# Where the small arithmetic of a layer normalisation runs: eight operations on GpSimd in the place of six on VectorE around one on GpSimd, in a four-layer graph kernel

## The chip, the cores and the metric

The kernel runs on one core of a Trainium2 chip. What counts is the device time of one execution in microseconds: 1110.71 us before the change, the median of three runs (1109.0 to 1111.08). In the profile the engines are PE (TensorE, with PEld for its weight loads), DVE (VectorE), ACT (ScalarE), POOL (GpSimd) and SP (SyncE, which issues transfers). L118 is line 118 of the kernel before.

## What is computed

A graph of 2708 nodes with 128 features each (x) and a sparse weighted adjacency (adj, 2708 × 2708) goes through four layers. Each layer is wrapped in the same way:

```
h = maximum(layernorm(x), 0)
x = x + layer(h)            # layers 0 to 3

layernorm(x) = (x - mean(x)) / sqrt(var(x) + 1e-5)     # over the 128 features of a node
```

- Layer 0: the transposed adjacency times h, over the degree.
- Layer 1: message passing. `gelu(s[i] + d[j] + b)` is weighted by `adj[i, j]` and summed over j, joined to h, taken through a linear map and gelu, added to h and normalised again with `ln_w` and `ln_b`.
- Layer 2: `adj @ h`, a linear map with relu, and a GRU cell.
- Layer 3: attention with two heads over the pattern of adj. Its input is normalised once more, and for each head `atten @ h + x` is normalised before a last linear map and elu; the heads are averaged.

So a node is normalised seven times: before each of the four layers, at the end of layer 1, at the start of layer 3's attention, and in layer 3 once for each head (two in one set of instructions).

## The kernel before

The nodes lie in 22 tiles of 128 rows (the last has 20), taken in groups of up to four: six groups, the last with two tiles. A row tile is [128 rows on partitions, 128 features]. x stays in on-chip memory as `xs`.

**A normalisation.** `moments` (L109–120) takes up to four row tiles: for each, VectorE computes mean and variance (`bn_stats`, `bn_aggr`, L116–117) into `mv` [128, k, 2]. L118 (VectorE) adds epsilon to the k variances, and L119 (GpSimd) raises that to the power −0.5. `factors` (L122–130) refines the result by one Newton step and makes the shift, −mean × rstd, with five instructions of VectorE (L125–129) on [128, k]. `scale_rows` (L132–135) then lets ScalarE write each row tile as func(scale × row + shift). The tiles `st`, `mv` and `r` come from the pool `small` with three buffers for each name. `moments` and `factors` are called apart, so that other work of VectorE lies between them while GpSimd takes the power:

- n0, before layer 0: `normalise` (L140), for the six groups one after another at the start.
- n1, before layer 1: `enter` adds layer 0's result to xs and calls `moments`; `rows` calls `factors` and `scale_rows` later.
- n1u, at the end of layer 1, and n2, before layer 2: steps 2–3 and 5–6 of `update` (L567–585); step 4 scales and lets GpSimd multiply by ln_w and add ln_b (L579).
- n3, before layer 3, and n3z, in its attention: in `finish_chunk` (L1023–1031), once for each of the six groups.
- n4, in layer 3: in `close` (L886–890), for two row tiles and both heads, twelve times.

In the trace the tiles of n0, n1, n2, n3 and n4 are all called n_r and n_mv; those of the other two n1u_r and n3z_r.

**The order of the work.** Layer 0 (0 to 245 us) is ordered by a scheduler: SyncE fetches rows of adj as `a`, TensorE multiplies them with h (L220) and transposes them (L249), and VectorE finds the nonzeros of each row in 22 blocks of 124 columns with `max` and an index search (L240, L241). GpSimd prepares for each tile the blocks at the diagonal (`near`, `dg`, L229–234). From there on the order is written by hand. The prologue of layer 1 (245 to 305) is a list of steps and tiles; `enter`, `rows` and `turn_rows` stand in it among steps that build the lists (L339 compares a list with a count, 128 x 2816). Layer 1 itself (to 640) runs in periods of one tile each: TensorE picks and sums (L499, L503, L524), ScalarE takes gelu, GpSimd and ScalarE write the matrices `put` (L423, L431), and `updates(t)` puts one step of an `update` in each period.

In layer 2 (to 860) TensorE multiplies chunks of 512 columns of the transposed adjacency with h (L959). At each piece, VectorE makes 0/1 masks of most row tiles and GpSimd of the rest (L951, L954). A generator, `finish_chunk`, lies over the products of the next chunk; its `yield n` means: go on after n more units of TensorE's work. The same holds for `close` in layer 3 (860 to 1108), which lies over the products of the attention: VectorE makes the weights (L806, 128 x 1024 in the wide runs), TensorE multiplies (L838), and a close divides by the sums and adds h (L884), normalises (n4), transposes (L894), multiplies (L903) and ends with elu, for which GpSimd runs L915–917 and VectorE L920–921.

Of the kernel before, what the change touches and what calls it, by code (L numbers as in the profile page):

```python
# [22 lines left out]
AF = mybir.ActivationFunctionType  # L23
ALU = mybir.AluOpType
# [15 lines left out]
EPS = 1e-5  # L40
# [20 lines left out]
def listed_layers(ctx: ExitStack, tc: tile.TileContext, x, adj, w, out, flag):  # L61
    nc = tc.nc
# [10 lines left out]
    xs = const.tile([P, NT, D], F32, name="xs")  # L73
    h = const.tile([P, NT, D], F32, name="hs")
# [31 lines left out]
    minus_half = const.tile([P, 8], F32, name="minus_half")  # L106
    nc.vector.memset(minus_half, -0.5)

    def moments(src, name, pool=small):  # L109

        k = len(src)
        st = pool.tile([P, k, 6], F32, name=name + "_st")
        mv = pool.tile([P, k, 2], F32, name=name + "_mv")
        r = pool.tile([P, 4, k], F32, name=name + "_r")
        for q in range(k):
            nc.vector.bn_stats(st[:, q, :], src[q])  # L116
            nc.vector.bn_aggr(mv[:, q, :], st[:, q, :])
        nc.vector.tensor_scalar(r[:, 3, :], mv[:, :, 1], EPS, None, ALU.add)  # L118
        nc.gpsimd.tensor_tensor(r[:, 0, :], r[:, 3, :], minus_half[:, 0:k], ALU.pow)  # L119
        return mv, r  # L120

    def factors(mv, r):  # L122

        rstd, shift, tmp, ve = (r[:, q, :] for q in range(4))
        nc.vector.tensor_tensor(tmp, rstd, rstd, ALU.mult)  # L125
        nc.vector.tensor_tensor(tmp, tmp, ve, ALU.mult)
        nc.vector.tensor_scalar(tmp, tmp, -0.5, 1.5, ALU.mult, ALU.add)
        nc.vector.tensor_tensor(rstd, rstd, tmp, ALU.mult)
        nc.vector.scalar_tensor_tensor(shift, mv[:, :, 0], -1.0, rstd, op0=ALU.mult, op1=ALU.mult)
        return rstd, shift  # L130

    def scale_rows(dst, src, rstd, shift, func):  # L132

        for q in range(len(src)):
            nc.scalar.activation(dst[q], src[q], func, bias=shift[:, q : q + 1], scale=rstd[:, q : q + 1])

    def tiles_of(v, t, k):
        return [v[:, t + q, :] for q in range(k)]

    def normalise(dst, src, t, k, func, name):  # L140

        rows = tiles_of(src, t, k)
        scale_rows(tiles_of(dst, t, k), rows, *factors(*moments(rows, name)), func)

    def span(t, k):

# [50 lines left out]
    with tc.tile_pool(name="l0c", bufs=1) as fix:  # L197
# [4 lines left out]
        with (  # L202
# [6 lines left out]
            for gi, (g0, gk) in enumerate(GROUPS):  # L209
# [4 lines left out]
                for q in range(gk):  # L214
                    n = g0 + q
                    m = size(n)
# [27 lines left out]
                for j in range(NT):  # L244
                    k = size(j)
                    p = bank("p_T")
                    for q in range(gk):
                        m = size(g0 + q)
# [52 lines left out]
    with (  # L301
# [27 lines left out]
        state = {}  # L329
# [215 lines left out]
        ups = {}  # L545

        def update(g, step):
            t, k = GROUPS[g]
            if step == 0:
                u = work.tile([P, 4, D], F32, name="u1")  # L550
                p = rpool.tile([P, CH], F32, tag="r", name="p_u")
                agg = aggs.pop(g)
                if size(t + k - 1) < P:
                    nc.vector.memset(u[:, k - 1, :], 0.0)
                for q in range(k):
                    m, c = size(t + q), (t + q) * P
                    pq = p[0:m, q * D : (q + 1) * D]
                    nc.tensor.matmul(pq, hT[:, c : c + m], upd_wT[:, 0, :], start=True, stop=False)
                    nc.tensor.matmul(pq, agg[:, q, 0:m], upd_wT[:, 1, :], start=False, stop=True)
                pv = p.rearrange("p (t d) -> p t d", t=4)  # L560
                bv = upd_b.unsqueeze(1).to_broadcast([P, 4, D])
                whole = k if size(t + k - 1) == P else k - 1
                nc.vector.tensor_tensor(u[:, 0:whole, :], pv[:, 0:whole, :], bv[:, 0:whole, :], ALU.add)
                if whole < k:
                    nc.vector.tensor_tensor(u[0:TAIL, whole, :], pv[0:TAIL, whole, :], upd_b[0:TAIL, :], ALU.add)
                ups[g] = [u]
            u = ups[g][0]  # L567
            rows = tiles_of(u, 0, k)
            if step == 1:
                nc.scalar.activation(u[:, 0:k, :], u[:, 0:k, :], AF.Gelu)  # L570
            if step == 2:
                nc.vector.tensor_tensor(u[:, 0:k, :], u[:, 0:k, :], h[:, t : t + k, :], ALU.add)  # L572
                ups[g].append(moments(rows, "n1u"))
            if step in (3, 6):
                ups[g].append(factors(*ups[g].pop()))
            if step == 4:
                scale_rows(rows, rows, *ups[g].pop(), AF.Identity)
                for v, op in ((ln_w, ALU.mult), (ln_b, ALU.add)):
                    nc.gpsimd.tensor_tensor(u[:, 0:k, :], u[:, 0:k, :], v.unsqueeze(1).to_broadcast([P, k, D]), op)  # L579
            if step == 5:  # L580
                nc.vector.tensor_tensor(xs[:, t : t + k, :], xs[:, t : t + k, :], u[:, 0:k, :], ALU.add)
                ups[g].append(moments(tiles_of(xs, t, k), "n2"))
            if step == 7:
                scale_rows(tiles_of(h, t, k), tiles_of(xs, t, k), *ups[g].pop(), AF.Relu)
                ups.pop(g)
# [75 lines left out]

        def rows(g):
            t, k = GROUPS[g]
            scale_rows(tiles_of(h, t, k), tiles_of(xs, t, k), *factors(*state.pop(("m", g))), AF.Relu)

        def turn_rows(g):
            t, k = GROUPS[g]
# [207 lines left out]
    def close(run, sums, first):  # L875

        res, inv3 = sums
        k0 = min(2, run[1] - first)
        t0 = run[0] + first
        n = 2 * k0  # L880
        att = out_pool.tile([P, 4, D], F32, name="att_s")
        for s in range(n):
            i = s % 2 * run[1] + first + s // 2
            nc.vector.scalar_tensor_tensor(  # L884
                att[:, s, :], res[:, i, 0:D], inv3[:, i : i + 1], h3[:, t0 + s // 2, :], op0=ALU.mult, op1=ALU.add
            )  # L886
        rows = tiles_of(att, 0, n)
        mv = moments(rows, "n4")
        yield 4.5
        scale_rows(rows, rows, *factors(*mv), AF.Identity)  # L890
        yield 4
        p = bank("p_aT")
        for s in range(n):
            nc.tensor.transpose(p[:, s * P : (s + 1) * P], att[:, s, :], ident)  # L894
        spend(0.25 * n)
        zT = out_pool.tile([P, 4, P], F32, name="z4T")
        nc.scalar.activation(
            zT[:, 0:n, :], p.rearrange("p (s i) -> p s i", s=4)[:, 0:n, :], AF.Identity, bias=shift2, scale=gain2
        )
        yield 1.5  # L900
        p = bank("p_o")
        for s in range(n):
            nc.tensor.matmul(  # L903
                p[:, s * D : (s + 1) * D], zT[:, s, :], ff1T[:, s % 2 * D : (s % 2 + 1) * D], start=True, stop=True
            )
        spend(0.33 * n)

        v = p.rearrange("p (q k d) -> p q k d", q=2, k=2)[:, 0:k0, :, :]
        el = out_pool.tile([P, 2, 2, D], F32, name="el")[:, 0:k0, :, :]
        po = out_pool.tile([P, 2, 2, D], F32, name="po")[:, 0:k0, :, :]  # L910
        nc.scalar.activation(el, v, AF.Relu, scale=-1.0)
        nc.scalar.activation(po, v, AF.Relu, scale=0.5)
        nc.scalar.activation(el, el, AF.Exp, scale=-1.0)
        less = out_pool.tile([P, 2, D], F32, name="less")
        nc.gpsimd.tensor_scalar(less[:, 0:k0, :], xs[:, t0 : t0 + k0, :], -1.0, None, ALU.add)  # L915
        nc.gpsimd.tensor_tensor(po[:, :, 0, :], po[:, :, 0, :], po[:, :, 1, :], ALU.add)
        nc.gpsimd.tensor_tensor(less[:, 0:k0, :], less[:, 0:k0, :], po[:, :, 0, :], ALU.add)
        yield 6
        y = out_pool.tile([P, 2, D], F32, name="y")
        nc.vector.tensor_tensor(el[:, :, 0, :], el[:, :, 0, :], el[:, :, 1, :], ALU.add)  # L920
        nc.vector.scalar_tensor_tensor(  # L921
            y[:, 0:k0, :], el[:, :, 0, :], 0.5, less[:, 0:k0, :], op0=ALU.mult, op1=ALU.add
        )
        for q in range(k0):
            m, i = size(t0 + q), (t0 + q) * P
            nc.sync.dma_start(out[i : i + m, :], y[0:m, q, :])
# [7 lines left out]
    with (  # L934
# [30 lines left out]
        def finish_chunk(t0, k0, pa):  # L965
# [8 lines left out]
            for t in range(t0, t0 + k0):  # L974
                m = size(t)
# [37 lines left out]
            for q in range(k0):  # L1013
                m = size(t0 + q)
# [8 lines left out]
            x_rows, h_rows = tiles_of(xs, t0, k0), tiles_of(h3, t0, k0)  # L1023
            mv = moments(x_rows, "n3")
            yield 6
            scale_rows(h_rows, x_rows, *factors(*mv), AF.Relu)
            yield 2
            mv = moments(h_rows, "n3z")
            yield 4
            z = zpool.tile([P, 4, D], F32, name="z3")  # L1030
            scale_rows(tiles_of(z, 0, k0), h_rows, *factors(*mv), AF.Identity)
            yield 4
            zT = zpool.tile([D, CH], F32, name="z3T")
            turn(
# [11 lines left out]
            for q in range(k0):  # L1046
                t = t0 + q
# [509 lines left out]
```

## Time and profile before

| what | before |
|---|---|
| time | 1110.71 us (1109.0 to 1111.08) |
| span of the profile | 1108.1 us |
| clock granted to TensorE | 0.933 |
| instructions of GpSimd | 466 |
| L118, n_r, 128 x 4 or 2 | 36, mean 178 ns |
| L125 to L129, n_r | 36 each, means 235, 198, 337, 233, 202 ns |
| L119, n1u_r and n3z_r, 128 x 4 | 5 and 5, means 1248 and 1768 ns |
| L806, weights of layer 3 | 176, 160.0 us |
| L423, put on GpSimd | 176, 147.7 us |

The page's second part cuts the span into 40 slices of 27.7 us. A digit is the busy share of a slice in tenths:

```profile
PE   3998887944389999999999979999979999999993
DVE  5999999997766668676887255655578977997673
POOL 4111111103385655776566253344310200340132
```

VectorE is full in slices 2 to 9, layer 0; TensorE in nearly all that come after the eleventh. A wait that the trace names stands in brackets behind a row of the timeline, as the idle time of the engine ahead of the instruction and what ended it.

### The profile page before, as it was taken

How to read it: one execution, taken by the hardware profiler on the slowest of the kernel's cores; microseconds unless marked ns; L12 is line 12 of the kernel's file. 1: busy time of each engine (PE TensorE's matmuls, PEld its weight loads, DVE VectorE, ACT ScalarE, POOL GpSimd, SP SyncE). 2: the span in 40 equal slices, each digit the busy share in tenths (PEclk: the TensorE clock that was granted, in tenths of full speed). 3: DMA queues.
4: the chain of work that ended last, by engine and by line, in shares of the span. 5: the costliest groups of instructions: out<-in, count | busy, mean ns of one | idle time of the engine just before them, and what ended most of it. 6: DMA issues, size and time to landing. Idle time of an engine off the chain costs nothing. (4 is left out here: it accounts for less than half of the span.)

```text
span 1108.1 us, 21904 instructions
## 1 busy us (share of the span) xinstructions
PE 963.6 (87%) x7968; PEld 760.1 (69%) x7968; DVE 839.4 (76%) x2948; ACT 504.2 (46%) x1319; POOL 394.1 (36%) x466
## 2 busy tenths in 40 slices
PE   3998887944389999999999979999979999999993
PEld 1455444523389999999898934444468899999772
DVE  5999999997766668676887255655578977997673
ACT  3857556623476666656676521433322200230142
POOL 4111111103385655776566253344310200340132
PEclk9999889755699999999999989999989999999996
DMA  9488978522133222322222056545300000000000
GB/s 361 164 299 281 324 259 288 178 64 68 46 106 102 96 86 90 106 86 101 83 103 80 28 193 209 190 157 198 100 18 1 1 9 1 1 20 1 2 15 14
DMA packets 55298, 125.39 MB, mean 113 GB/s; under 512 B 7414, under 2 KB 19782, under 8 KB 52472
## 3 DMA queue, kind: packets, MB, share of 16 engines
q1 hardware_dynamic: 48590, 121.12, 31.6%
q10 hardware_dynamic: 6590, 2.77, 1.0%
q8 instruction: 64, 1.05, 0.4%
q14 instruction: 54, 0.44, 0.1%
HBM read 77.30 MB, written 30.84 MB: 98 GB/s over the span
## 5 line engine op out<-in xcount | busy, mean ns | idle before, releaser
L838 PE MATMUL att<-hv,wt 128*128 128x129 f32 (+2 forms) x1936 | 240.7, 281 | 9.2 <-DVE wt L806 9.2
L838 PEld LDWEIGHTS att<-hv,wt 128*128 128x128 f32 (+2 forms) x1936 | 221.8, 190 | 26.2 <-DVE wt L806 9.1
L806 DVE SCALAR_TENSOR_TENSOR wt<-row,lift,mask 128x1024 f32<-128x1024 f32 (+5 forms) x176 | 160.0, 939 | 34.2 <-PE att L838 34.2
L423 POOL TENSOR_SCALAR put<-mine,value 128x128 f32<-128x128 bf16 x176 | 147.7, 855 | 72.4 <-DVE mine L339 70.0
L499 PE MATMUL p_m<-s,sel 128*128 128x128 bf16 x1452 | 160.8, 219 | 5.4 <-ACT g L511 5.4
L119 POOL TENSOR_TENSOR n_r<-n_r,minus_half 128x4 f32<-128x4 f32 (+1 forms) x36 | 51.3, 1425 | 316.1 <-DVE n_r L118 305.2
L503 PE MATMUL p_m<-d,cols 124*128 124x128 bf16 (+1 forms) x1452 | 161.0, 219 | 1.4 <-DVE cols L453 1.3
L220 PE MATMUL acc<-a,hs 128*128 128x512 f32 (+2 forms) x264 | 122.3, 599 | 27.6 <-DMA a<-in_adj 18.9
L524 PE MATMUL agg<-put,g 128*128 128x128 f32 (+1 forms) x968 | 135.8, 281 | 0.0
L241 DVE FIND_INDEX8 col<-val,a 128x8 uint16<-128x124 f32 (+1 forms) x441 | 118.6, 280 | 0.0
L959 PE MATMUL p_agg<-a,hs 128*128 128x512 f32 (+2 forms) x264 | 111.5, 564 | 7.7 <-DVE u L572 4.8
L524 PEld LDWEIGHTS agg<-put,g 128*128 128x128 f32 x968 | 118.1, 192 | 0.0
L499 PEld LDWEIGHTS <-sel 128*128 128x128 bf16 x1452 | 103.7, 97 | 10.8 <-issue 7.1
L503 PEld LDWEIGHTS <-cols 124*128 124x128 bf16 (+1 forms) x1452 | 101.8, 97 | 1.9 <-DVE cols L453 1.9
L240 DVE MAX8 val<-a 128x8 f32<-128x124 f32 (+1 forms) x441 | 102.6, 272 | 0.0
L511 ACT ACTIVATE g<-p_m 128x512 f32<-128x512 f32 x132 | 73.0, 553 | 63.6 <-PE p_m L503 63.6
L431 ACT ACTIVATE put<-mine,value 128x128 f32<-128x128 bf16 x308 | 100.5, 390 | 0.0
L220 PEld LDWEIGHTS acc<-a,hs 128*128 128x128 f32 (+1 forms) x264 | 49.7, 209 | 72.2 <-issue 43.4
L249 PEld LDWEIGHTS p_T<-ident,a 128*128 128x128 f32 x484 | 59.0, 146 | 52.8 <-ACT aT L253 25.4
L249 PE MATMUL p_T<-ident,a 128*128 128x128 f32 x484 | 77.7, 293 | 18.3 <-DMA a<-in_adj 10.0
L253 ACT ACTIVATE aT<-p_T 128x512 f32<-128x512 f32 (+2 forms) x132 | 70.9, 541 | 40.0 <-issue 16.3
L959 PEld LDWEIGHTS p_agg<-a,hs 128*128 128x128 f32 (+1 forms) x264 | 48.6, 196 | 56.6 <-issue 55.1
(228 smaller groups left out, 1396.6 us busy)
## 6 DMA issues: line engine op xcount, KB each, us to landing
a<-in_adj SPq DMA_DIRECT2D x21, 1354.0 KB
adjT<-aT SPq DMA_DIRECT2D x105, 256.0 KB
a<-adjT SPq DMA_DIRECT2D x20, 1280.0 KB
spread<-passed SPq DMA_DIRECT2D x22, 704.0 KB
later<-sel SPq DMA_DIRECT2D x22, 616.0 KB
later<-sel SPq DMA_DIRECT2D x22, 82.5 KB
adjT<-aT SPq DMA_DIRECT2D x21, 74.0 KB
a<-adjT SPq DMA_DIRECT2D x4, 370.0 KB
```

The source lines that it names most:

```text
L220: nc.tensor.matmul(accs[ci][:, 0:cw], h[0:m, n, :], a[0:m, c : c + cw], start=(n == 0), stop=(n == NT - 1))
L240: nc.vector.max(val[:, n, b, :], ab)
L241: nc.vector.max_index(col[:, n, b, :], val[:, n, b, :], ab)
L249: nc.tensor.transpose(p[0:k, q * P : q * P + m], a4[0:m, q, j * P : j * P + k], ident[0:m, 0:m])
L423: nc.gpsimd.tensor_scalar(st["put", 0][:, b, :], st["mine"][:, b, :], st["value"][:, b : b + 1], None, ALU.mult)
L431: nc.scalar.activation(st["put", 1][:, b - HP, :], st["mine"][:, b, :], AF.Identity, scale=st["value"][:, b : b + 1])
L499: nc.tensor.matmul(p[:, b - b0, :], st["sel"][:, b, :], s3[:, q, t % 2, :], start=(q == 0), stop=False)
L503: nc.tensor.matmul(p[:, b - b0, :], st["cols"][0:kb, b, :], d3[0:kb, b, q, :], start=False, stop=(q == 2))
L524: nc.tensor.matmul(agg, g[:, b - 4 * k, :], put, start=(b == 0), stop=False)
L806: nc.vector.scalar_tensor_tensor(wt[0:kj, :], row[0:kj, k, c : c + n], lift[0:kj, j, k : k + 1], mask[0:kj, j, c : c + n], op0=ALU.max, op ...
L838: nc.tensor.matmul(banks[s // 3][0:m, s % 3, :], wt[0:kj, q * P : q * P + m], hv[0:kj, j, k, :], start=(v < 2 and s // 3 not in touched), ...
L959: nc.tensor.matmul(pa[:, 0:n], h[0:k, j, :], a[0:k, j - j0, 0:n], start=(j == 0), stop=(j == NT - 1))
```

## The change

`moments` now also does the work of `factors`, all of it on GpSimd, and hands back scale and shift: add epsilon, power, three instructions that form 1.5 − 0.5 × rstd² × (var + eps), the multiplication with it, mean × rstd, and the sign. VectorE's combined last instruction (L129) becomes two of GpSimd. `factors` and its calls disappear; `scale_rows` stands where it stood. The purpose is to take small dependent instructions off VectorE and to have one crossing from VectorE to GpSimd and one from there to ScalarE, in the place of VectorE to GpSimd to VectorE to ScalarE. Each GpSimd instruction waits for the one before it on GpSimd's own semaphore.

```diff
@@ moments
-        nc.vector.tensor_scalar(r[:, 3, :], mv[:, :, 1], EPS, None, ALU.add)
-        nc.gpsimd.tensor_tensor(r[:, 0, :], r[:, 3, :], minus_half[:, 0:k], ALU.pow)
-        return mv, r
-
-    def factors(mv, r):
 
         rstd, shift, tmp, ve = (r[:, q, :] for q in range(4))
-        nc.vector.tensor_tensor(tmp, rstd, rstd, ALU.mult)
-        nc.vector.tensor_tensor(tmp, tmp, ve, ALU.mult)
-        nc.vector.tensor_scalar(tmp, tmp, -0.5, 1.5, ALU.mult, ALU.add)
-        nc.vector.tensor_tensor(rstd, rstd, tmp, ALU.mult)
-        nc.vector.scalar_tensor_tensor(shift, mv[:, :, 0], -1.0, rstd, op0=ALU.mult, op1=ALU.mult)
+        nc.gpsimd.tensor_scalar(ve, mv[:, :, 1], EPS, None, ALU.add)
+        nc.gpsimd.tensor_tensor(rstd, ve, minus_half[:, 0:k], ALU.pow)
+        nc.gpsimd.tensor_tensor(tmp, rstd, rstd, ALU.mult)
+        nc.gpsimd.tensor_tensor(tmp, tmp, ve, ALU.mult)
+        nc.gpsimd.tensor_scalar(tmp, tmp, -0.5, 1.5, ALU.mult, ALU.add)
+        nc.gpsimd.tensor_tensor(rstd, rstd, tmp, ALU.mult)
+        nc.gpsimd.tensor_tensor(shift, mv[:, :, 0], rstd, ALU.mult)
+        nc.gpsimd.tensor_scalar(shift, shift, -1.0, None, ALU.mult)
         return rstd, shift
@@ normalise; rows, close and finish_chunk (n3, n3z) in the same way
-        scale_rows(tiles_of(dst, t, k), rows, *factors(*moments(rows, name)), func)
+        scale_rows(tiles_of(dst, t, k), rows, *moments(rows, name), func)
@@ update
-            if step in (3, 6):
-                ups[g].append(factors(*ups[g].pop()))
```

More of the change, by code (lines that the diff above doesn't have):

```diff
@@ L663, in rows @@
             t, k = GROUPS[g]
-            scale_rows(tiles_of(h, t, k), tiles_of(xs, t, k), *factors(*state.pop(("m", g))), AF.Relu)
+            scale_rows(tiles_of(h, t, k), tiles_of(xs, t, k), *state.pop(("m", g)), AF.Relu)
         def turn_rows(g):
@@ L889, in close @@
         yield 4.5
-        scale_rows(rows, rows, *factors(*mv), AF.Identity)
+        scale_rows(rows, rows, *mv, AF.Identity)
         yield 4
@@ L1025, in finish_chunk @@
             yield 6
-            scale_rows(h_rows, x_rows, *factors(*mv), AF.Relu)
+            scale_rows(h_rows, x_rows, *mv, AF.Relu)
             yield 2
@@ L1030, in finish_chunk @@
             z = zpool.tile([P, 4, D], F32, name="z3")
-            scale_rows(tiles_of(z, 0, k0), h_rows, *factors(*mv), AF.Identity)
+            scale_rows(tiles_of(z, 0, k0), h_rows, *mv, AF.Identity)
             yield 4
```

## The prediction

> **What bounds the kernel now.** I read the page first (busy shares, slices), then busy time by stage, then rows, waits and timelines of the stages where the change sits. From the page:
>
> ```profile
> PE 963.6 (87%) x7968; PEld 760.1 (69%) x7968; DVE 839.4 (76%) x2948; ACT 504.2 (46%) x1319; POOL 394.1 (36%) x466
> L806 DVE SCALAR_TENSOR_TENSOR wt<-row,lift,mask 128x1024 f32<-128x1024 f32 (+5 forms) x176 | 160.0, 939 | 34.2 <-PE att L838 34.2
> L119 POOL TENSOR_TENSOR n_r<-n_r,minus_half 128x4 f32<-128x4 f32 (+1 forms) x36 | 51.3, 1425 | 316.1 <-DVE n_r L118 305.2
> ```
>
> GpSimd looks idle (36%), but that is an average. Busy time by stage (start and end, length, then busy us of each engine):
>
> ```profile
> 0.00:245.00 245.00, 187.51 (x756) 108.31 (x757) 232.06 (x1568) 145.50 (x338) 39.27 (x83) 0.89 0.71 250
> 245.00:305.00 60.00, 24.69 (x144) 19.10 (x144) 47.41 (x154) 23.82 (x57) 17.61 (x21) 0.59 0.17 57
> 305.00:640.00 335.00, 323.08 (x4506) 312.26 (x4503) 233.35 (x455) 215.90 (x628) 208.89 (x262) 1.00 0.26 88
> 670.00:800.00 130.00, 129.11 (x352) 59.93 (x351) 74.62 (x207) 45.95 (x113) 50.64 (x31) 1.00 0.51 170
> 860.00:1084.00 224.00, 220.09 (x1799) 202.23 (x1798) 179.04 (x333) 44.10 (x92) 48.34 (x42) 0.98 0.02 6
> ```
>
> Layer 0 (to 245) is bound by VectorE (232 of 245); the prologue of layer 1 (245 to 305) is a latency chain that VectorE dominates; everything from 305 to 1084 is bound by TensorE, except 640–670 and 800–860. Only the first two can sell a VectorE saving; in the others only a longer chain counts, and only where its slack ends. A normalisation in layer 2, from the timeline at 690 us (start, length, row):
>
> ```profile
> 690.13 0.17 DVE L118 TENSOR_SCALAR n_r<-n_mv 128x4 f32<-128x4 f32 x1
> 690.20 1.22 DVE L951 TENSOR_SCALAR mask<-a 128x2048 uint8<-128x2048 f32 x1
> 690.38 1.93 POOL L119 TENSOR_TENSOR n_r<-n_r,minus_half 128x4 f32<-128x4 f32 x1 [10.85 <-DVE n_r L118]
> 692.35 0.57 DVE L125 TENSOR_TENSOR n_r<-n_r 128x4 f32<-128x4 f32 x1 [0.92 <-POOL n_r L119]
> 693.55 0.16 DVE L129 SCALAR_TENSOR_TENSOR n_r<-n_mv,n_r 128x4 f32<-128x4 f32 x1
> ```
>
> and in layer 3, beside the weights L806:
>
> ```profile
> 870.49 0.17 DVE L118 TENSOR_SCALAR n_r<-n_mv 128x4 f32<-128x4 f32 x1
> 870.56 2.48 DVE L806 SCALAR_TENSOR_TENSOR wt<-row,lift,mask 128x1024 f32<-128x1024 f32 x2
> 870.74 1.97 POOL L119 TENSOR_TENSOR n_r<-n_r,minus_half 128x4 f32<-128x4 f32 x1 [30.27 <-DVE n_r L118]
> 873.74 0.16 DVE L129 SCALAR_TENSOR_TENSOR n_r<-n_mv,n_r 128x4 f32<-128x4 f32 x1
> 874.58 0.30 PE L894 MATMUL p_aT<-ident,att_s 128*128 128x128 f32 x1 [0.58 <-ACT att_s L135]
> ```
>
> The power takes 1.93–1.97 us here; three in a row with VectorE off the memory took 3.23 (12.72–15.95), so 1.01 is its own. It gets going only as the VectorE instruction that started before it ends (691.42; 871.80), and then needs some 0.9.
>
> **What the Trainium skill says.** "SBUF — State Buffer", "Who interferes with whom": GpSimd's port pair is shared with VectorE; an instruction of VectorE with two inputs in SBUF, or a tensor_scalar in a two-port mode, and a reading one of GpSimd shut each other out whole, by issue order. The trace agrees (1.01 becomes 1.93 and 1.97). "GPSIMD Engine Reference", "3.1 Elementwise", has two dispatch hops on GpSimd against one on VectorE; the trace has no tiny GpSimd multiply, but one of 128x20 takes 0.23 us and VectorE's of 128x4 take 0.16.
>
> **The change part by part.** *Removed:* six VectorE instructions (118, 125–129) in each of 48 normalisations (36 whose tile is called n_r, six n1u_r, six n3z_r), 288 in all, some 60 us of busy time; 0.15–0.17 us each where nothing disturbs them, five at a pitch of 0.20, so about 1.2 us per normalisation, and one crossing back from GpSimd to VectorE. *Added:* GpSimd's add ahead of the power and six instructions behind it, each waiting for the one before. Step: below by VectorE's pitch, 0.20; above by 0.40 (a 128x128 tensor_scalar, 0.53, less some of its size). I take 0.27: the 128x20 multiply's 0.19–0.23 and the 0.04–0.08 us seen between dependent GpSimd instructions (916 to 917: 0.08). Alone, a chain is 0.2 + 1.01 + 6 × 0.27 = 2.8, and with the start 3.1 us; before, 0.17 + 0.1 + 1.01 + 5 × 0.2 + gaps = 2.5. *Moved:* outside layer 0 the order on TensorE, ScalarE and the queues is as before; whatever stood behind the power on GpSimd now stands behind the chain.
>
> By stage:
> - Layer 0: the chains run while VectorE does lists. VectorE saves six sets of small instructions (those of groups 3–5 lie between list instructions at a pitch of some 0.1, so 18 × 0.1 = 1.8), their waits for the power (0.74, 0.67, 0.36) and a step blocked to 18.62; but its first block maxima wait for near and dg, which stand behind three chains on GpSimd. The first hs goes from 19.46 to about 26, which TensorE's slack (11.8 us of waiting at the end) takes. −1.5 (−4 to +1).
> - Prologue: six groups × 1.1 us leave VectorE, but ScalarE takes rows in order, behind copies that wait for other VectorE work, so little of it arrives; and group 5's factors no longer stand behind L339 (297.21 to 298.83); still L339 has two inputs and holds up the rest of that chain. TensorE waits 30.7 us for hs in all. −1.5 (−4 to +1).
> - Layer 1, 305–640: a chain in GpSimd's queue delays the puts (L423) by 3 us; GpSimd waits 70 us there for mine, and no product waits for a put (0.0), so it is hidden. −0.5.
> - 640–670: behind one another on GpSimd stand the chains of n1u of group 5 and n2 of group 4, then ln_w and ln_b of group 5, the memset of score (657.07) and the masks; the masks release the pieces of adjT that TensorE waits for at 665.7. Two chains less two powers, 3.4, less the VectorE part that was on this way: +2.1 (0 to +4).
> - Layer 2: n3 above lasts 690.10 to 693.71 = 3.6. After: the mask to 691.35, then 2.8 = 694.15: +0.45. n3z follows on it with the same +0.5 and, by the rest of a mask, 0.1 more. TensorE waits for z already at p_z (0.24 at 701.57) and is in order: 1.1 × 4 chunks = +4.5 (+1 to +7).
> - 800–860: the mask of 20x148 comes behind a chain (+1.7 to L977 and the weights); relief of VectorE gives 2.2. −0.5 (−3 to +2).
> - Layer 3: in the first close the bn_aggr ends at 870.45; the weights hold the first step to 871.8 and the power to 873.0 (done 873.9); with the factors gone VectorE goes on with two more weights, so steps 3 and 4 get in at 874.3 and 875.5, the last four by 876.6, against 873.90: +2.7, and TensorE already waits 0.58. The same walk gives +0.8, 0, 0, +2, +2.7 for the next closes and 0 for the later ones, which have 1.4–3.6 us of slack: 8.2 if each step is held up so. I take two thirds, since VectorE pauses for TensorE (34.2 us): +5.5 (0 to +9).
> - Tail, where nothing hides anything: the last but one chain starts when its bn_aggr ends (1087.05) and, with some 0.4 us behind two-input work, ends near 1090.2, about where L129 does (1090.47); the last (128x2, power 0.70) can only start then and takes 0.2 + 0.7 + 6 × 0.27 = 2.5 to 1092.7, against 1091.61 before: +1 (0 to +2).
>
> Sum: −1.5 − 1.5 − 0.5 + 2.1 + 4.5 − 0.5 + 5.5 + 1 = +9.1: 1119.8 us.
>
> **The rivals.** *Relief wins.* For: VectorE is full in layer 0 (232 of 245) and the prologue, and a crossing goes. Against: a third of the saving only lies there. With −4 and −4 there, −2 in 800–860, +1, +2 and +1 in 640–670, layer 2 and layer 3, and −0.5 and +1 as above, −6.5: 1104. *A draw.* Steps at 0.20 and chains that slip into VectorE's pauses: 640–670 +1, layer 2 +2, layer 3 +1, the rest as above: +1.0, so 1111.7. *Shut out everywhere.* All eight steps wait for a VectorE instruction, 8 × 1.24 = 10 us beside weights, and in the closes with slack too: layer 3 +15, layer 2 +6, the rest as above: +20, so 1131. For it: the power does so in every close; against: L916 and L917 take 0.84 and 0.86 where 0.72 is their own, so many get through.
>
> **How the numbers follow.** The forecast 0.53, shut out 0.13, relief 0.19, draw 0.15. Faster 0.20, same 0.15, slower 0.65. The range runs from 1105, near relief's 1104, to 1130, near shut-out's 1131; half of each of these cases, 0.09 and 0.07, lies beyond. My ends of the stages would sum to a wider span, but they won't all fall on one side.
>
> **What would show it.** GpSimd's steps at 0.27 pitch where VectorE is quiet; n3 and n3z 0.5 us longer each and p_z's wait 1 us longer per chunk; the chain of the first close over 5.5 us and p_aT 2–3 us later; VectorE some 60 us less busy and TensorE's busy time the same. I am wrong if steps take 0.4 or more (then 1125 and up), if the first hs at 26 us is more than layer 0 can take back, or if layer 0 and the prologue end 5 us or more sooner.

## The result, and the profile after

The changed kernel takes 1122.26 us (median of four runs, 1120.11 to 1125.58) against 1110.76 before: a ratio of 1.0109, 95% interval [1.008, 1.0138], so some 12 us slower (9 to 15). Forecast were +9.1 us and 1105 to 1130. Runs of one kernel spread by a few us, and a profile shows one of them; that of the changed kernel is its longest, 1125.58 us (span 1123.7 against 1108.1 in the profile before). All shifts below that come from a profile are shifts of that run.

The page of the changed kernel, rows that answer to those shown of the kernel before (L802 is L806 before; L120 is the chain's first step):

```profile
PE 977.3 (87%) x7968; PEld 769.0 (68%) x7968; DVE 786.0 (70%) x2660; ACT 504.5 (45%) x1319; POOL 485.6 (43%) x802
L802 DVE SCALAR_TENSOR_TENSOR wt<-row,lift,mask 128x1024 f32<-128x1024 f32 (+5 forms) x176 | 158.1, 925 | 48.5 <-PE att L834 48.5
L120 POOL TENSOR_SCALAR n_r<-n_mv 128x4 f32<-128x4 f32 (+1 forms) x36 | 22.4, 623 | 278.0 <-DVE n_mv L117 271.7
```

VectorE is 53 us less busy, GpSimd 92 us more. TensorE has the same 7968 products, and yet 13.7 us more of busy time: a first sign of something the forecast didn't have. By stage, in the columns of before (start and end, length, busy us of each engine, granted clock, share of transfers, GB/s):

```profile
0.00:245.00 245.00, 188.57 (x750) 108.60 (x750) 227.03 (x1530) 144.00 (x330) 47.00 (x125) 0.89 0.70 248
245.00:305.00 60.00, 28.24 (x150) 20.64 (x151) 41.51 (x119) 25.52 (x67) 29.36 (x63) 0.56 0.20 64
305.00:640.00 335.00, 324.31 (x4513) 313.60 (x4512) 226.85 (x407) 216.65 (x632) 231.26 (x318) 1.00 0.26 88
670.00:800.00 130.00, 126.86 (x324) 58.13 (x324) 59.95 (x157) 39.90 (x102) 58.74 (x78) 0.97 0.51 174
860.00:1084.00 224.00, 219.32 (x1794) 205.22 (x1793) 170.09 (x283) 38.70 (x86) 61.17 (x98) 0.97 0.02 5
```

In layer 2 the clock is 0.97 where it was 1.00. A normalisation there, from the timeline of the changed kernel (first chunk; L947 is L951 before, L133 is L135):

```profile
691.58 1.19 DVE L947 TENSOR_SCALAR mask<-a 128x2048 uint8<-128x2048 f32 x1
691.74 1.11 POOL L120 TENSOR_SCALAR n_r<-n_mv 128x4 f32<-128x4 f32 x1 [10.05 <-DVE n_mv L117]
692.94 1.03 POOL L121 TENSOR_TENSOR n_r<-n_r,minus_half 128x4 f32<-128x4 f32 x1
694.05 0.20 POOL L122 TENSOR_TENSOR n_r<-n_r 128x4 f32<-128x4 f32 x1
694.33 0.20 POOL L123 TENSOR_TENSOR n_r<-n_r 128x4 f32<-128x4 f32 x1
695.46 0.24 POOL L127 TENSOR_SCALAR n_r<-n_r 128x4 f32<-128x4 f32 x1
695.73 1.65 ACT L133 ACTIVATE h<-xs,n_r 128x128 f32<-128x128 f32 x4 [10.56 <-POOL n_r L127]
```

The mask shuts out the first step (1.11 us for an instruction of 0.2), the power has its own 1.03, and the rest go at a pitch of 0.28: 694.05, 694.33, and 695.46 for the sixth. From the end of the last bn_aggr to ScalarE's first row it takes 4.06 us for n3 where it took 3.65, and 4.49 for n3z where it took 3.71 (most chunks): +1.2 per chunk, where the forecast had 1.1. What TensorE makes of that, two chunks later (p_z takes the transposes of z, the rows that n3z scales):

```profile
768.03 1.65 ACT L133 ACTIVATE z<-h,n3z_r 128x128 f32<-128x128 f32 x4 [5.06 <-POOL n3z_r L127]
768.57 1.51 PE L151 MATMUL p_z<-ident,z 128*128 128x128 f32 x4 [0.58 <-ACT z L133]
```

It waits 0.58 us for the first row of z and goes on row by row (1.51 for four transposes that take 0.60 when all is there, and 0.95 to 1.04 in these chunks of the kernel before). Right behind it, in busy time by stretch of the changed kernel (the figure after the engines is the granted clock):

```profile
739.20:769.90 30.70, 29.72 (x78) 13.46 (x77) 15.07 (x39) 9.00 (x27) 12.02 (x19) 1.00 0.41 143
769.90:773.30 3.40, 3.40 (x9) 1.85 (x9) 0.00 (x0) 1.74 (x3) 3.11 (x3) 0.50 0.62 170
```

For 3.4 us the clock is 0.5. The same happens at 735.8 and 804.0, behind the other two waits; the kernel before has none of the three.

To see where the time goes, each TensorE product of the changed kernel can be laid beside the same product before. The shift, at products that stood at these times before:

| before, us | stage that ends there | shift after | stage gave | forecast |
|---|---|---|---|---|
| 304 | layer 0 and prologue | −0.1 | −0.1 | −3.0 |
| 640 | periods of layer 1 | −1.3 | −1.1 | −0.5 |
| 672 | into layer 2 | +1.6 | +2.8 | +2.1 |
| 801 | layer 2 | +11.5 | +9.9 | +4.5 |
| 860 | last chunk, first weights | +11.0 | −0.5 | −0.5 |
| 1084 | layer 3 | +14.9 | +3.9 | +5.5 |
| end | tail | +15.6 | +0.7 | +1.0 |

The first row is the least certain: two kernels below that are the changed kernel up to 640 us, the one with late transposes and the one with all masks of layer 2 on VectorE, stand at −0.3 and −5.4 at 304 in their profiles.

### The profile page after: what moved, and what is told of

It is laid out like the page before. It is cut to its first block, busy times and chain, and to the rows that moved or that the text cites. A ratio compares the mean times of both kernels' runs of the same rounds, so it can differ in the third digit from the quotient of the medians.

```text
span 1123.7 us, 21993 instructions
## 1 busy us (share of the span) xinstructions
PE 977.3 (87%) x7968; PEld 769.0 (68%) x7968; DVE 786.0 (70%) x2660; ACT 504.5 (45%) x1319; POOL 485.6 (43%) x802
## 5 line engine op out<-in xcount | busy, mean ns | idle before, releaser
L834 PEld LDWEIGHTS att<-hv,wt 128*128 128x128 f32 (+2 forms) x1936 | 224.5, 192 | 25.5 <-issue 6.6
L802 DVE SCALAR_TENSOR_TENSOR wt<-row,lift,mask 128x1024 f32<-128x1024 f32 (+5 forms) x176 | 158.1, 925 | 48.5 <-PE att L834 48.5
L421 POOL TENSOR_SCALAR put<-mine,value 128x128 f32<-128x128 bf16 x176 | 142.7, 827 | 48.5 <-DVE mine L337 42.7
L120 POOL TENSOR_SCALAR n_r<-n_mv 128x4 f32<-128x4 f32 (+1 forms) x36 | 22.4, 623 | 278.0 <-DVE n_mv L117 271.7
L955 PE MATMUL p_agg<-a,hs 128*128 128x512 f32 (+2 forms) x264 | 114.4, 577 | 10.7 <-DMA a<-adjT 10.7
```

What stands on the lines that cost most here:

```text
L421: nc.gpsimd.tensor_scalar(st["put", 0][:, b, :], st["mine"][:, b, :], st["value"][:, b : b + 1], None, ALU.mult)
L802: nc.vector.scalar_tensor_tensor(wt[0:kj, :], row[0:kj, k, c : c + n], lift[0:kj, j, k : k + 1], mask[0:kj, j, c : c + n], op0=ALU.max, op ...
L834: nc.tensor.matmul(banks[s // 3][0:m, s % 3, :], wt[0:kj, q * P : q * P + m], hv[0:kj, j, k, :], start=(v < 2 and s // 3 not in touched), ...
L955: nc.tensor.matmul(pa[:, 0:n], h[0:k, j, :], a[0:k, j - j0, 0:n], start=(j == 0), stop=(j == NT - 1))
```

## The experiments

Theory 1 is the prediction's working. Theory 2, formed from the table: layer 2 costs what it does because a wait of TensorE is followed by a stretch of low clock that costs as much again; and layer 0 doesn't gain, because its slack was less than the late first hs. The ratios are to runs of the kernel before on the same chip.

**One stage at a time.** Four kernels have the chain for some of the seven normalisations, and are the kernel before otherwise. Each is the same edit with another set of names:

```diff
+    CHAINED = ("n3", "n3z",)      # or ("n4",), ("n1u", "n2"), ("n0", "n1")
     def moments(src, name, pool=small):
...
+        if name in CHAINED:
+            (the eight GpSimd instructions of the changed kernel)
+            return None, (rstd, shift)
         nc.vector.tensor_scalar(r[:, 3, :], mv[:, :, 1], EPS, None, ALU.add)
...
     def factors(mv, r):
+        if mv is None:
+            return r
```

Layer 2 alone (n3, n3z):

> The kernel before, with the chain on GpSimd only for n3 and n3z (layer 2). Theory 1 (steps as the prediction worked them out: 1.1 us of wait per chunk and nothing else): +4.5 us, about 1115. Theory 2 (read off the two traces laid product by product: every wait of TensorE for z of a microsecond or more is followed by a stretch of 3.41 us at a granted clock of 0.5, which costs as much again): +8 to +10 us, about 1119.5, with stretches at 0.5 near 730-810 that the kernel before has not. Theory 3 (the loss comes from the late start of layer 2, behind n1u and n2): below +2 us.

1118.32 us, ratio 1.0072 [1.0059, 1.0085]: +8.0. Its products shift by 1.1, 3.0, 2.9 and 2.8 us in the four chunks, and its clock falls to 0.5 at 736, 770 and 804, as in the changed kernel. Its start into layer 2 is on time, so theory 3 falls. Theory 2 had the size, with waits at p_z of 0.74, 0.60 and 0.61 us.

Layer 3 alone (n4):

> The kernel before, with the chain only for n4 (the closes of layer 3 and the tail). Theory 1: +5.5 for the closes and +1 for the tail, about 1117. Theory 2: the first close waits 2.3 us longer and loses 1.7 us more to the clock, the close that waited in the kernel before (983) gains 1.3, the tail costs 0.7: +3.5 us, about 1114. Theory 3 (shut out by the weights at every step): +10 us or more.

1111.32 us, ratio 1.002 [1.001, 1.003]: +2.2, less than either. Its 22 runs fall in two groups, fourteen of 1109.65 to 1112.05 us and eight of 1114.46 to 1116.49; the profile is of one of the longer (1115.28), and none shows a shorter one. The first close of that run, from the timeline (L821 weights, L122 to L129 the chain, L909 the transposes):

```profile
870.76 4.84 DVE L821 SCALAR_TENSOR_TENSOR wt<-row,lift,mask 128x1024 f32<-128x1024 f32 x4
870.93 1.18 POOL L122 TENSOR_SCALAR n_r<-n_mv 128x4 f32<-128x4 f32 x1 [30.08 <-DVE n_mv L119]
872.19 1.91 POOL L123 TENSOR_TENSOR n_r<-n_r,minus_half 128x4 f32<-128x4 f32 x1
874.18 0.28 POOL L124 TENSOR_TENSOR n_r<-n_r 128x4 f32<-128x4 f32 x1
874.54 1.12 POOL L125 TENSOR_TENSOR n_r<-n_r 128x4 f32<-128x4 f32 x1
876.86 1.65 ACT L150 ACTIVATE att_s<-att_s,n_r 128x128 f32<-128x128 f32 x4 [14.33 <-POOL n_r L129]
877.41 1.58 PE L909 MATMUL p_aT<-ident,att_s 128*128 128x128 f32 x4 [3.03 <-ACT att_s L150]
```

With VectorE's small instructions gone, four weights follow without a pause, and the chain gets one of its first four steps in at each end of one, as the forecast walked it; the last four follow behind the weights at 0.28. TensorE waits 3.03 us where it waited 0.58, +2.8 at p_aT, and a stretch of half clock behind it (879 to 882) makes +4.6, with 0.4 from ahead of layer 3. But then nothing more is lost in closes: the one that before waited 1.06 us at 983 even gets back 1.8 us. Its chain is held up by the weights too (from the last bn_aggr to ScalarE's first row 7.2 us, 978.43 to 985.61, where it had been 5.1), but TensorE now comes 4.6 us later and these statistics only 0.7, so there is time for it. A further 1.9 us go at 1035, where a stretch of half clock lasts 6.83 us for the 3.41 of before, and 1.3 in the tail.

The end of layer 1 alone (n1u, n2):

> The kernel before, with the chain only for n1u and n2 (the updates at the end of layer 1 and the way into layer 2). Theory 1: -0.5 in the periods and +2.1 at 640-670: +1.6 us, about 1112.3. Theory 2: -1.3 in the periods and +3.1 at 640-670, of which 1.7 are a second stretch at clock 0.5: +1.8 us. Theory 3 (hidden): no change.

1111.65 us, ratio 1.0015 [1.0008, 1.0021]: +1.7. The periods give 0.8 up to 639 us, as in the changed kernel (−1.1), but it is gone at 641 (+0.1), since the half clock in which both kernels go over to layer 2 begins at 638.6 in the place of 642.6. The way into layer 2 costs 3.0 in the profiled run, and its clock is 0.5 from 666 to 673, 6.8 us for the 3.4 of before. So of the 3.0 some 1.7 is clock; the other 1.3 is put down to the queue on GpSimd, which no run takes apart.

The start alone (n0, n1):

> The kernel before, with the chain only for n0 and n1 (start of layer 0, prologue of layer 1). Theory 1: the relief of VectorE pays in both stages: -3 us, about 1107.7. Theory 2: the first products start 5 us later and layer 0's transposes end 13 us later, which eats what the prologue gains: within 1 us of the kernel before, with the first p_m at 304 in both.

1108.43 us, ratio 0.9983 [0.9976, 0.999]: −1.9, between the two. The four add up to +10.0, beside the 12 of the whole change: the costs stand side by side.

**What makes the loss in layer 2.** First, the transposes of z four units of TensorE's work later, in the changed kernel:

```diff
             scale_rows(tiles_of(z, 0, k0), h_rows, *mv, AF.Identity)
-            yield 4
+            yield 8 if t0 < 16 else 4
```

> The changed kernel (all chains on GpSimd), with the transposes of z four units of TensorE's work later in chunks 0 to 3 (the yield ahead of them 8 in the place of 4), nothing else. Theory 2 (the waits for z and the clock's stretches after them are the loss in layer 2): the idle gaps of 0.6-0.9 us at p_z and the three stretches of 3.41 us at 0.5 go, 6 to 7 us less than the changed kernel: about 1115.5. Rival (the loss is GpSimd and VectorE in each other's way, so it shows up at the next product that needs them): no more than 2 us less, about 1121.

1117.74 us, ratio to before 1.0073 [1.0049, 1.0096]: some 4 us of the 12 are back, by the medians; the intervals of the two kernels overlap. In the profile the gaps at p_z and the stretches behind them are gone, and layer 2 shifts by 3.6 us in the place of 9.9: the 6 us that theory 2 had, in the stage. TensorE still waits, but elsewhere: 0.61 and 0.54 us at p_m for ScalarE, 1.82 and 0.48 at p_agg for transfers, and behind none of these is there a stretch. Two us of the 6 are not seen in the time; the run profiled has a stretch at half clock at 563 to 567, in the periods of layer 1, behind a wait of 2.08 us, and is 2.0 us behind the changed kernel's ahead of layer 2.

Then useless work where TensorE waited, in the kernel with the chain in layer 2 only:

```diff
+            if 0 < t0 < 16:
+                p = bank("p_fill")
+                for _ in range(3):
+                    nc.tensor.matmul(p[:, 0:n], W_msgT, hc[:, 0:n], start=True, stop=True)
             zT = zpool.tile([D, CH], F32, name="z3T")
```

> The kernel with the chain only in layer 2, with three products of 128x128x512 that nobody reads put ahead of the transposes of z in chunks 1 to 3, so that TensorE works where it waited (its result is the same). Theory 2 (a wait of TensorE is followed by a stretch at half clock): the three stretches go, and with them 3 x 1.7 = 5 us, though TensorE does 3.9 us more work: about 1113.5. Rival (the stretches have another cause, or cost nothing by themselves): 1118.3 as before or up to 4 us more.

1116.69 us, ratio 1.0063 [1.005, 1.0076]: −1.0 against the kernel without the filling (between −3 and +1 by the two intervals), not −5. In busy time by stretch, that kernel and then the filled one:

```profile
735.80:739.10 3.30, 3.30 (x8) 1.80 (x9) 0.80 (x1) 1.14 (x2) 2.13 (x1) 0.51 1.02 373
769.90:773.30 3.40, 3.40 (x6) 1.41 (x6) 0.00 (x0) 1.43 (x3) 2.70 (x2) 0.52 0.72 223
804.00:807.40 3.40, 3.40 (x9) 2.25 (x9) 0.00 (x0) 1.28 (x4) 1.36 (x3) 0.52 0.81 214
```

```profile
735.80:739.10 3.30, 3.30 (x11) 1.48 (x11) 0.60 (x1) 1.90 (x4) 2.51 (x2) 1.00 0.98 359
769.90:773.30 3.40, 3.40 (x12) 1.57 (x11) 0.00 (x0) 2.62 (x5) 1.95 (x2) 1.00 0.95 313
804.00:807.40 3.40, 3.40 (x12) 1.66 (x11) 0.00 (x0) 2.22 (x5) 1.03 (x2) 1.00 0.44 114
```

The three stretches are gone. What was wrong was the price of the filling: a product of 128x128x512 in 32 bits is two records of 0.43 us each (six from 732.43 to 735.01), so three take 2.58 us per chunk, not 1.29. That is 1.4 more than the 1.2 of waiting they replace: 3 × 1.4 = 4.1 lost, 3 × 1.7 = 5.1 of clock won: −1.0, which agrees with the measured one. Had the stretches cost nothing, it would be +4.1, outside what was measured.

Then the converse: the kernel before, with its arithmetic as it was, and a wait made by the order alone:

```diff
             scale_rows(tiles_of(z, 0, k0), h_rows, *factors(*mv), AF.Identity)
-            yield 4
+            yield 2 if 0 < t0 < 16 else 4
```

> The kernel before, all its arithmetic where it was, with the transposes of z in chunks 1 to 3 two units of TensorE's work earlier (the yield ahead of them 2 in the place of 4), so that TensorE gets there 0.4 to 0.9 us before z is there and waits, with no part of the change in the kernel. Theory 2 (a wait of this size by itself is followed by 3.41 us at clock 0.5): 0.4 to 0.9 us of wait and 1.7 us of clock in each of three chunks, +5 to +8 us, with stretches behind each p_z: about 1116. Rival (the stretches come with GpSimd's work or by chance): only the waits, +1 to +2.5 us, about 1111.5.

1117.15 us, ratio 1.0064 [1.005, 1.0079]: +7.1, in the range of theory 2, without a GpSimd step more. But the run profiled is one of 1112.92 us: it waits 1.10, 0.71 and 1.30 us at p_z, and has no stretch behind any of them. The first wait, and the busy time and clock of the stage:

```profile
729.85 1.48 PE L153 MATMUL p_z<-ident,z 128*128 128x128 f32 x4 [1.10 <-ACT z L135]
670.00:800.00 130.00, 125.88 (x333) 57.12 (x332) 74.19 (x207) 42.49 (x108) 50.19 (x31) 1.00 0.50 167
```

This run loses 5.3 us in layer 2 all the same, 3.1 of it in the waits and 1.4 in transposes that come row by row. Another run took 1113.03; the other four took 1116.92 to 1118.21. The gap of some 4.5 us is about three stretches of 1.7, but none of the four longer runs has a profile. So a wait of this size is enough to lose 7 us on the median, and that a stretch follows it is likely, not certain.

How much of it is the number of steps? The chain in layer 2 with four steps; it leaves out the Newton step:

```diff
-            nc.gpsimd.tensor_tensor(tmp, rstd, rstd, ALU.mult)
-            nc.gpsimd.tensor_tensor(tmp, tmp, ve, ALU.mult)
-            nc.gpsimd.tensor_scalar(tmp, tmp, -0.5, 1.5, ALU.mult, ALU.add)
-            nc.gpsimd.tensor_tensor(rstd, rstd, tmp, ALU.mult)
```

> The kernel with the chain only in layer 2, with the four instructions of the Newton step left out of it (the refinement of rstd is not computed), so the chain has four steps. If the length of the chain makes the waits: 4 x 0.28 = 1.1 us less per chain, z some 2.2 us earlier per chunk, about as early as in the kernel before, no stretches: 1110 to 1111.5. Rival (what counts is that GpSimd's first step is shut out by VectorE's masks, or stands behind its own masks): most of the loss stays, 1115 or more.

1107.41 us, ratio 0.9978 [0.997, 0.9986]: 10 us less than with eight steps, and 2.4 less than before, more than expected. From statistics to rows n3 takes 2.95 us (4.07 with eight steps) and n3z 3.37 (4.50): 1.12 each, four pitches of 0.28. So with a full chain it is the four steps that put z behind TensorE; the shut-out of the first steps is still in this kernel, and z is in time all the same.

Last, the queue on GpSimd: the changed kernel with GpSimd's masks on VectorE.

```diff
-                nc.gpsimd.tensor_scalar(
+                nc.vector.tensor_scalar(
                     mask[0:m, j0 + most, c : c + n], a[0:m, most, 0:n], 0.0, None, ALU.is_gt
```

> The changed kernel, with GpSimd's masks of layer 2 (L950 of the changed kernel, one row tile in five) on VectorE. If the chain of n3z is late because it stands behind these masks in GpSimd's queue (first step at 729.9, 1.6 us after its statistics): n3z some 1.3 us earlier in chunks 1 to 3, and the masks ahead of layer 3 earlier; waits at p_z gone: 6 to 10 us less than the changed kernel, 1112 to 1116. Rival (the eight steps and the shut-out by VectorE's masks): VectorE's masks are longer, so no gain or a loss: 1121 to 1125.

1119.44 us, ratio 1.0089 [1.0074, 1.0104], 2 to 3 us less than the changed kernel by the medians, though the intervals overlap. It isn't in layer 2: that stage shifts by 11.7 us in its profile (9.9 in the changed kernel), with 4.35 to 4.96 us for n3 and 4.45 to 5.5 for n3z. The stage from 801 to 860, where a mask on GpSimd stood behind a chain, gains 3.4 more. So taking GpSimd's masks out of its queue does not help layer 2; what the queue alone costs stays open, since this edit gives VectorE more masks, and n3 takes longer by it (4.35 us for 4.06).

**Layer 0 and the prologue.** The chain for n0 alone and for n1 alone:

> The kernel before, with the chain only for n0 (ahead of layer 0). Theory 2: VectorE's lists end 3.4 us earlier (240.9 in the place of 244.3), but TensorE's first products start 5.5 us later (hs at 25 for 19.5), its transposes end after the lists (241 to 247, by how the transfers and the clock fall), and layer 1's first product of rows waits for them: no gain on the mean, 1109 to 1111, with a wider scatter than the kernel before. Theory 1 (VectorE bounds layer 0): -3.4 us, about 1106.5.

1110.72 us, ratio 1.0009 [1.0001, 1.0018]: +1.0. VectorE's lists end at 241.0 (244.3 before), but hs comes at 25.0 (19.5), TensorE's transposes end at 244.6 (233.4), and layer 1's first product starts at 245.4 (245.2). In the changed kernel VectorE ends its lists at 240.9 and then stands still; from its waits at 240 to 250 us:

```profile
DVE some L331 <- ACT aT L251: 5.8, 1, 5.8
PE p_r L346 <- DVE rows_n L333: 0.8, 1, 0.8
```

The first layer-1 instruction of VectorE waits 5.8 us for ScalarE's copies of the late transposes, and TensorE, which before waited 11.8 us for VectorE here, waits 0.8. The bound of the stage has changed hands. Not in every run, though: in the profile of the kernel with all masks of layer 2 on VectorE, which is the changed kernel up to here, the transposes end at 241.6 and layer 1 begins at 242.4, 2.8 us sooner than before.

> The kernel before, with the chain only for n1 (prologue of layer 1). Theory 2: the whole gain of the start is here, since between the first product of rows (245) and the first p_m (304) the kernel with both chains gains 2.5 us: -2 to -2.5 us, about 1107.7. Theory 1: -1.5 us, 1108.4. Rival (the prologue is latency bound and L339 shuts the chain out): no change.

1107.33 us, ratio 0.9979 [0.997, 0.9988]: −2.3. All that the start gains, it gains in the prologue.

Then the chain where it takes work off a full VectorE and nobody waits for it: n1, and groups 3 to 5 of n0.

```diff
-        scale_rows(tiles_of(dst, t, k), rows, *factors(*moments(rows, name)), func)
+        scale_rows(tiles_of(dst, t, k), rows, *factors(*moments(rows, name, chain=t >= 12)), func)
```

> The kernel before, with the chain for n1, and for n0 only in groups 3 to 5, whose small instructions lie among VectorE's list work; groups 0 to 2, which the first products wait for, as before. Theory 2 (the late first hs is what spoils layer 0): first hs back at about 19.5, lists end about 2 us earlier than in the kernel before, transposes in time; with n1 -4 to -4.5 us, about 1105.7. Rival (the saving in layer 0 is made in groups 0 to 2): as n1 alone.

1103.02 us, ratio 0.9942 [0.9928, 0.9955]: 6.5 us less than before, more than expected and the best of all kernels here. hs comes at 19.8, the lists end at 240.9, the transposes at 235.5, and layer 1's first product starts at 241.8 in the place of 245.2; the prologue gains a further 2.8 (p_m at 297.8 for 304.1). In the prologue VectorE is busy for 38.33 us (47.41 before), in busy time by stage of this kernel:

```profile
245.00:305.00 60.00, 30.34 (x216) 23.50 (x215) 38.33 (x104) 28.38 (x72) 36.94 (x71) 0.64 0.17 55
```

So the whole of VectorE's gain in layer 0, 3.4 us, comes with the three late groups; the early ones added only the late start.

## Why the prediction was right, and where its steps were not

The direction, the size (+9.1 for 12, 9 to 15) and the range held. By its steps:

- **The step of 0.27 us** was right: 0.28. So was the shape of a chain in layer 2, n3 +0.45 forecast and +0.41 measured. n3z was forecast at +0.6 and took +0.78.
- **Layer 2, +4.5 (+1 to +7)**: l2_only gives +8.0, above the range. The mechanism was right, z comes late and TensorE takes it in order. The step "1.1 us × 4 chunks" failed in size: three of the chunks cost 2.8 to 3.0, about 1.2 for the late z and 1.7 for 3.4 us at half clock. The term that was missing is the clock; "TensorE's busy time the same" was the sign for it, and it rose by 13.7 us. The 1.2 came out right in part by luck. The "0.24 at 701.57" is a gap ahead of a weight load, and no product at p_z waits in the kernel before: there was some slack, so the waits are only 0.6 to 0.9, and the rest is transposes that come row by row (1.5 us for 1.0).
- **640–670, +2.1**: +1.7 in time, +2.8 to +3.0 in the profiles, right in size by luck: a stretch of clock gave 1.7, and only 1.3 is left for the queue. Two chains less two powers are 3.6 by the prediction's own steps, not 3.4.
- **Layer 0, −1.5 (−4 to +1)**: wrong in sign, +1.0 with n0 alone, as in the prediction's own sign of being wrong, a first hs too late for layer 0 to take back. The step that failed is "which TensorE's slack (11.8 us of waiting at the end) takes". It was read from the run in which the transposes end earliest, and it isn't all there: in eight profiles with n0 as before the transposes end at 233.4 to 239.6, 237.0 on the mean, and in five with the chain for all of n0 at 241.6 to 246.9, 244.9 on the mean. So they move by 7.9 us where the first hs moves by 5.5, the lists that they should lie under end 3.4 sooner (240.9), and VectorE needs the transposed copies before it can go on: the bound changes hands before any gain is left, in four of these five profiles. Why they move by more than hs wasn't tried.
- **Prologue, −1.5 (−4 to +1)**: −2.3 with n1 alone, within the range. The comparison L339 does hold up the chain of group 5, but in one step alone (1.44 us for 0.2, at 295.10 in that kernel's profile), and the chain ends at 297.14 where L129 ended at 299.70.
- **800–860, −0.5**: −0.5, of which the mask behind a chain was forecast at +1.7 and VectorE's relief at −2.2; in l2_only the shift goes up by 1.7 to 12.6 at the first weights and down by 2.2 after them.
- **Layer 3, +5.5 (0 to +9)**: +2.2 with the tail (forecast +6.5), +3.9 in the profile of the changed kernel. The first close was right in both profiles (+2.7, then +2.7 and +2.8), which are of longer runs. "The same walk gives … +2, +2.7 for the next closes" failed: it took each close by itself, while a TensorE that is already late gives the later chains slack. A loss in a chain of stages isn't added at each of them. Why fourteen of the 22 runs lose less still, though the first close should cost them 2.7 too, stays open.
- **The rivals**: "relief wins" had the right place in the prologue; "shut out everywhere" was seen at the first four steps of the first close, and later closes, with chains of up to 7.2 us, cost nothing. The terms given for "relief wins" sum to −5.5, not −6.5, so 1105.

That the number came so near is in part luck. By the four kernels with one stage each, layer 2 cost 3.5 us more than forecast (the clock) and the start gave 1.1 less, while layer 3 with the tail cost 4.3 less: errors that nearly cancel.

## What to carry to other kernels

Move small dependent work to a slow engine only where the engine it leaves is full and nobody waits for the result soon: the same chain was worth −6.5 us in n1 and the late groups of n0, and cost 8 us in layer 2, where TensorE had hardly any slack behind it. Price each stage by its own slack, and let a delay in one stage give slack to the next. Where TensorE is full and an operand comes late, look at the granted clock behind the wait before blaming contention: here 1.2 us of delay cost up to 3.0.

## What the runs showed of the hardware that was not expected

- Behind waits of TensorE of 0.6–0.9 us, followed by transposes that come row by row, the granted clock was 0.5 for 3.4 us, in three chunks of the changed kernel and of l2_only; with TensorE kept busy through the same place it was 1.00. A wait alone doesn't do it. Three waits of 0.7–1.3 us in the profiled run of the kernel before with early transposes had no such stretch, nor had two of four at p_z in the kernel with all masks on VectorE (0.56 and 0.79; those of 1.94 and 2.07 had one). Nor had two of 1.46 us, at 498.5 and 561.7, in layer 1 of the kernel before. And a stretch with no wait just ahead is seen too (946 to 950 in the kernel before, where TensorE is busy through the 3.4 us before it).
- In each of the 14 profiles all stretches of half clock begin on one grid of 3.413 us (735.76, 769.90 and 804.03 in the changed kernel lie ten steps apart) and last one step or more. The grid lies differently in each profile, so one and the same wait falls differently on it from run to run. That may be why runs of one kernel fall in groups; it wasn't tried. How busy TensorE is in the step ahead doesn't sort the cases: 69 to 78% before the three stretches of the changed kernel, 62 to 74% at the three waits with early transposes, without one. What decides it stays open.
- GpSimd's multiply of 128x4 takes 0.20 us and the next one that depends on it starts 0.28 after it, hardly behind VectorE (0.16 at a pitch of 0.20). Of the two dispatch hops, against one of VectorE, that the Trainium skill counts for GpSimd ("GPSIMD Engine Reference", "3.1 Elementwise") no more than the 0.08 us between the two pitches shows.
- Beside weights of VectorE without a pause, GpSimd gets in one instruction at the end of each (1.18, 1.91, 0.28, 1.12 us for steps of 0.2, 1.0, 0.2, 0.2). This agrees with the Trainium skill ("SBUF — State Buffer", "Who interferes with whom"), by which an instruction of VectorE with two inputs in SBUF contends with one of GpSimd that reads it. But the power, once it has got going, runs beside the next weights: it ends at 874.10, and the four weights from 870.76 to 875.60 take 1.21 us each without a pause.
